# Low-rank stage: two-bank gelus, a moved output step, an x product on TensorE and a new split of the final sums

## The chip, the cores and the metric

The kernel runs on one core of a Trainium2 chip. The metric is device time in microseconds (us) from start to end of one execution. Before the change it is 999.62 us, the median of 3 runs (998.93 to 999.8).

A core has a matmul engine (TensorE, "PE" in the profile; "PEld" is its weight load), a vector engine (VectorE, "DVE"), an activation engine (ScalarE, "ACT"), a general engine (GpSimd, "POOL") and a sync engine (SyncE, "SP"). Each works through its own queue of instructions in order. Matmul results land in PSUM, which has eight banks of 128 partitions by 512 fp32 numbers here. Transfers to and from memory are issued by SP or ACT and run on 16 DMA engines.

## What is computed

Two layers with residuals over x of shape (32, 128, 128) in fp32:

```
x = x + L0_ffn(L0_cond(x, cond))     # mixtures of experts
x = x + L1_ffn(L1_cond(x, cond))
# L1_cond: shared silu experts + 8 routed gelu experts, weighted and summed
# L1_ffn, the low-rank stage:
P = x @ U1                 # 128 -> 32
H = gelu(P @ V1 + b1)      # 32 -> 512, tanh form of gelu
Q = H @ U2                 # 512 -> 32
out = Q @ V2 + b2          # 32 -> 128
```

The kernel folds U1 into the last weights of L1_cond, so that the experts' outputs are summed straight into P.

## The kernel before, in words

The 4096 tokens stand in 8 blocks (NB) of 512 columns (TB), with the 128 features on the partitions. Four blocks make a superblock (SB = 4), so there are two superblocks (NS = 2). All of x stays in SBUF (xT, later called x1T).

The work goes through stages. In L0 each shared unit (shared_up, L255) and each pair unit (pair_up, L429) multiplies into four PSUM tiles and takes a gelu of each (hidden, L239). Then comes the FFN: 8 blocks by 8 experts make 64 units (ffn_up, L615), each with four chunks. A chunk makes a tile g (gate) and a tile u (up) with by_columns (L217, matmul at L222); ScalarE takes silu of g (L569), VectorE multiplies it by u (L570). VectorE then forms four sums of the results (L630 to L633), and ffn_down (L640) projects.

In L1 the units stand in one list (`units`, L844 to L851): shared units "s", routed units "r" and low-rank units "l", each for a superblock. `pipelined` (L186) emits up(next unit), then down(this unit), then `after` for this unit.

A low-rank unit (sb, c) handles chunk c of the 512 hidden features for the four blocks of a superblock. low_up (L816) makes for each block a matmul with a contraction of 32 into its own PSUM tile ul, in its own quarter of the array's rows (L822), and a gelu of 128x512 (L823). low_down (L826) sums the four blocks' projections into the tile q_ps, a quarter of the array's columns each (`into`, L768, matmul at L771). When chunk 3 is done, low_out (L831) copies q_ps to qT (L833), multiplies by V2 for each block into o_ps (L837), adds b2 and x on VectorE (L839, tile fin), and stores: blocks 0 and 2 are issued on SyncE, blocks 1 and 3 on ScalarE (L841). The tail of the list runs: routed units 2 to 7 of superblock 1, then ("l", 0, 3), then the four ("l", 1, c). low_out(0) follows down("l", 0, 3), thus after up("l", 1, 0); low_out(1) comes last.

PSUM is shared out by tag: mm_tile (L107) gives one of six single-bank tiles in turn, y_tile (L110) one of two more for sums. A new tile of a tag waits until the last reader of an earlier one is done with it. The order of instructions on each engine is made by a planner: it follows program order as priority, and lets a later instruction go first when the earlier one is not ready in its own reckoning. It then sets every wait.

Of the kernel before, what the change touches and what calls it, by code (L numbers as in the profile page):

```python
# [44 lines left out]
SB = 4  # L45
NS = NB // SB
NT = B * S // P
H = 512
NC = H // P
# [28 lines left out]
def columns(cols):  # L78
    out, at = {}, 0
    for name, n in cols:  # L80
        out[name] = slice(at, at + n)
        at += n
    return out, at
# [3 lines left out]
AT32, NCOLS32 = columns(COLS32)  # L87
# [5 lines left out]
def adaln_ffn(  # L93
# [3 lines left out]
    nc = tc.nc  # L97
    V = nc.vector
# [4 lines left out]
    work = ctx.enter_context(tc.tile_pool(name="work", bufs=2))  # L103
    dram = ctx.enter_context(tc.tile_pool(name="dram", bufs=1, space=bass.MemoryType.DRAM))
    psum = ctx.enter_context(tc.tile_pool(name="psum", bufs=1, space=bass.MemoryType.PSUM))

    def mm_tile(name):  # L107
        return psum.tile([P, TB], F32, tag="mm", name=name, bufs=6)

    def y_tile(name):  # L110
        return psum.tile([P, TB], F32, tag="y", name=name, bufs=2)

    def const(shape, name, dtype=F32):
        return cpool.tile(shape, dtype, tag=name, name=name)
# [3 lines left out]
    par32 = const([P, NCOLS32], "par32")  # L118
# [11 lines left out]
    ident = const([P, P], "ident")  # L130
# [17 lines left out]
    for to, w in zip(downs_t, (s_w2, r_w2[: E1 // 2], r_w2[E1 // 2 :])):  # L148
        n = w.shape[0]
        nc.sync.dma_start(out=to.rearrange("p (e f) -> p e f", e=n), in_=w.rearrange("e d f -> d e f"))  # L150

    def col(name, i=0, n=1):
        return par[:, AT[name].start + i : AT[name].start + i + n]
# [85 lines left out]
    def hidden(ps, h, rhs, w, bias, unit):  # L239

        for c in range(NC):
            before("up", *unit, c)
            nc.tensor.matmul(ps[c], lhsT=w[:, c * P : (c + 1) * P], rhs=rhs, start=True, stop=True)  # L243
            nc.scalar.activation(h[:, c, :], ps[c], AF.Gelu_apprx_tanh, bias=bias[:, c : c + 1])  # L244
# [9 lines left out]

    def shared_up(blk):  # L255
        h = work.tile([P, NC, TB], F32, tag="h", name=f"hs0_{blk}", bufs=3)
        ps = [mm_tile(f"us_{blk}_{c}") for c in range(NC)]
        hidden(ps, h, xT[blk], sw1_t, col("sb1", 0, NC), ("s", blk))
        if blk < 2:
            for b in range(4 * blk, 4 * blk + 4):  # L260
                sums(b)
        return h
# [143 lines left out]
    def fetch(q):  # L406

        if q % 4 == 0:
            batch["e"] = registers(expert_at, q, mybir.EngineType.SP, (E0 - 1) * P)
        w = wpool.tile([P, NPCOLS], F32, tag=f"w{q % NW}", name=f"w_{q}")  # L410
        nc.sync.dma_start(out=w, in_=experts[bass.ds(batch["e"][q % 4], P), :])
        weights[q] = w
# [14 lines left out]
    def pair_up(q):  # L427
        if q + NW - 1 < NPAIR:
            fetch(q + NW - 1)  # L429
        if q + AHEAD < NPAIR:  # L430
            gather(q + AHEAD)
        w, x = weights[q], slots.pop(q)
        h = work.tile([P, NC, 2 * S], F32, tag="h", name=f"h0_{q}", bufs=3)
        ps = [mm_tile(f"u_{q}_{c}")[:, : 2 * S] for c in range(NC)]
        hidden(ps, h, x.rearrange("p s t -> p (s t)"), w[:, ATP["w1"]], w[:, ATP["eb1"]], ("p", q))
        return h

# [97 lines left out]
    held, in_dram, fgates = {}, {}, {}  # L535
# [64 lines left out]
    def gate_ahead(i):  # L600

        if i < len(ffn_units):
            blk, e = ffn_units[i]
            g, k = divmod(e, 4)
            bcast[i] = spread(fgates[blk][32 * k : 32 * k + 1, g, :], f"fg_{blk}_{e}")
# [9 lines left out]
    def ffn_up(blk, e):  # L615
        i = blk * EF + e
        gate_ahead(i + 2)
        input_ahead(i + 1)
        h = work.tile([P, NC, TB], F32, tag="h", name=f"hf_{blk}_{e}", bufs=3)
        cg = gated.pop((blk, e))  # L620
        for c in range(NC):
            cs = slice(c * P, (c + 1) * P)
            g, u = mm_tile(f"g_{blk}_{e}_{c}"), mm_tile(f"u_{blk}_{e}_{c}")
            by_columns(g, wg_t[:, e, cs], c0T[blk], D // 2)
            by_columns(u, wu_t[:, e, cs], cg, D // 2)
            glu(g, u, h[:, c, :], f"sf_{blk}_{e}_{c}")
        b11, b12, b21, b22 = (h[:, k, n] for k in (slice(0, 2), slice(2, 4)) for n in (slice(0, HALF), slice(HALF, TB)))
        t = work.tile([P, 3, 2, HALF], F32, tag="bsum", name=f"t_{blk}_{e}", bufs=2)
        t2, t3, t4 = (t[:, j] for j in range(3))
        V.tensor_tensor(t3, b22, b12, ALU.subtract)  # L630
        V.tensor_tensor(b12, b12, b11, ALU.subtract)  # L631
        V.tensor_tensor(t2, b22, b12, ALU.subtract)  # L632
        V.tensor_tensor(t4, t2, b21, ALU.subtract)  # L633
        if blk == 0:
            a_prepare(e)
        if rest:
            rest.pop(0)()
        return b11, b12, b21, b22, t2, t3, t4
# [115 lines left out]
    x1T = xT  # L754
# [13 lines left out]
    def into(y, w, h, first, last):  # L768

        for j in range(SB):  # L770
            nc.tensor.matmul(y[32 * j : 32 * (j + 1), :], lhsT=w, rhs=h[:, j, :], start=first, stop=last)  # L771

    def sh_up(sb, k):
        e, c = divmod(k, 2)
        h = work.tile([P, SB, TB], F32, tag="h", name=f"hs_{sb}_{k}", bufs=3)
        for j in range(SB):
            x = x1T[SB * sb + j]
            g, u = mm_tile(f"g1_{sb}_{k}_{j}"), mm_tile(f"u1_{sb}_{k}_{j}")
            by_columns(g, sws_t[0][:, e, c, :], x, 32)
            by_columns(u, sws_t[1][:, e, c, :], x, 32)  # L780
            glu(g, u, h[:, j, :], f"s1_{sb}_{k}_{j}")
        return h
# [13 lines left out]
    def r_up(sb, e):  # L796
        h = work.tile([P, SB, TB], F32, tag="h", name=f"hr_{sb}_{e}", bufs=3)
        g, k = divmod(e, 4)
        for j in range(SB):
            gate = spread(grows[sb][32 * k : 32 * k + 1, g, j * TB : (j + 1) * TB], f"rg_{sb}_{e}_{j}")  # L800
            ps = mm_tile(f"ur_{sb}_{e}_{j}")
            by_columns(ps, rw1_t[:, e, :], x1T[SB * sb + j], 32)
            a = work.tile([P, TB], F32, tag="sg", name=f"ar_{sb}_{e}_{j}", bufs=4)
            nc.scalar.activation(a, ps, AF.Gelu)  # L804
            V.tensor_tensor(h[:, j, :], a, gate, ALU.mult)  # L805
        return h
# [9 lines left out]
    def low_up(sb, c):  # L816
        h = work.tile([P, SB, TB], F32, tag="h", name=f"hl_{sb}_{c}", bufs=3)
        at = AT32["v1"].start + c * P
        for j in range(SB):
            ps = mm_tile(f"ul_{sb}_{c}_{j}")  # L820
            own = slice(32 * j, 32 * (j + 1))
            nc.tensor.matmul(ps, lhsT=par32[own, at : at + P], rhs=held["p", sb][own, :], start=True, stop=True)  # L822
            nc.scalar.activation(h[:, j, :], ps, AF.Gelu_apprx_tanh, bias=col("b1", c))  # L823
        return h

    def low_down(sb, c, h):  # L826
        if c == 0:
            held["q", sb] = y_tile(f"q_ps{sb}")
        into(held["q", sb], col("u2", c * 32, 32), h, c == 0, c == NC - 1)

    def low_out(sb):  # L831
        q = work.tile([P, TB], F32, tag="lgT", name=f"qT{sb}", bufs=1)
        V.tensor_copy(q, held["q", sb])  # L833
        for j in range(SB):
            ps = mm_tile(f"o_ps{sb}_{j}")
            own = slice(32 * j, 32 * (j + 1))
            nc.tensor.matmul(ps, lhsT=par32[own, AT32["v2"]], rhs=q[own, :], start=True, stop=True)  # L837
            t = work.tile([P, TB], F32, tag="fin", name=f"fin{sb}_{j}", bufs=4)
            V.scalar_tensor_tensor(t, ps, col("b2"), x1T[SB * sb + j], ALU.add, ALU.add)  # L839
            queue = nc.sync if j % 2 == 0 else nc.scalar  # L840
            queue.dma_start(out=out[SB * sb + j], in_=t)  # L841

    STAGES = {"s": (sh_up, sh_down), "r": (r_up, r_down), "l": (low_up, low_down)}
    units = [("s", sb, k) for sb in range(NS) for k in range(4)]  # L844
# [8 lines left out]
    def after(kind, sb, i):  # L853
        if (kind, sb, i) == ("s", 0, 0):
            gate_rows(0)

            l1_scores(1)
        if (kind, sb, i) == ("s", 0, 2):
            route(1)
        if (kind, sb, i) == ("s", 1, 0):  # L860
            gates_to_dram("r", 1)
            gate_rows(1)
        if kind == "r" and i == E1 - 1:
            low_in(sb)
        if (kind, sb, i) == ("l", 0, NC - 1):
            low_out(0)

    def unit_up(kind, *at):
# [4 lines left out]

    pipelined(units, unit_up, unit_down, after)
    low_out(1)


# [80 lines left out]
```

## Time and profile before

| What | us |
|---|---|
| median of 3 runs | 999.62 |
| the profiled execution, device time | 998.32 |
| its span, first to last record | 996.6 |
| TensorE matmul busy | 983.5 |
| VectorE busy | 634.3 |
| ScalarE busy | 353.2 |
| gelus of the low-rank stage (L823), 32 of 128x512, mean each | 0.696 |
| table loads on ScalarE for L823, 2, mean each | 1.283 |
| sums fin (L839), 8, mean each | 0.742 |
| silu in the FFN (L569), 256, mean each | 0.598 |
| product in the FFN (L570), 256, mean each | 0.686 |

In the profile a group of instructions is written as line, engine, operation, output <- inputs, shapes and count. In a timeline the first two columns are the start and the length in us; instructions of one group that follow each other are merged, and the brackets hold the idle time of the engine ahead of them and what ended it. "L841 ACTq" is the issue of a transfer from ScalarE's queue. Ends of matmuls are modelled, so starts are the better measure.

### The profile page before, as it was taken

Reading aid. Unit: us, or ns where it says so; the run is one execution under the profiler, and the core shown is the slowest. Engines: PE = TensorE matmul, PEld = TensorE weight load, DVE = VectorE, ACT = ScalarE, POOL = GpSimd, SP = SyncE. Lnnn points to the kernel's source line nnn. Section 1 sums busy time; section 2 is a strip of 40 time slices with the busy share of each in tenths; the row PEclk is TensorE's granted clock in tenths of the full one; section 3 lists DMA queues with packets and bytes.
Section 4 is the critical chain, followed back from the end, with each engine's and each line's share of the span. In section 5 each row is a group of like instructions: output and inputs, shape, how many; then the busy total and the mean of one; then the engine's idle time right before and its main releaser. Section 6 shows DMA issues by size and latency. Waiting matters only on the chain.

```text
span 996.6 us, 15169 instructions
## 1 busy us (share of the span) xinstructions
PE 983.5 (99%) x5998; PEld 465.0 (47%) x5998; DVE 634.3 (64%) x1126; ACT 353.2 (35%) x615; POOL 142.0 (14%) x145
## 2 busy tenths in 40 slices
PE   8999999999999999999999999999999999999996
PEld 3588886344444444444444444444444443323341
DVE  4444445667685676686676687668667656638593
ACT  5355445323232232232232323223223223335764
POOL 0000000210010101010101010101010001009780
PEclk9999999999999999999999999999999999999999
DMA  9555551000000000000000000000000000000002
GB/s 331 179 169 172 179 173 46 26 1 1 4 1 1 1 1 2 1 1 1 1 2 1 1 1 4 1 2 1 1 1 1 1 1 4 1 7 2 1 2 85
DMA packets 18743, 35.10 MB, mean 35 GB/s; under 512 B 1696, under 2 KB 9888, under 8 KB 18656
## 3 DMA queue, kind: packets, MB, share of 16 engines
q1 hardware_dynamic: 17808, 32.61, 10.3%
q10 hardware_dynamic: 864, 1.52, 0.4%
q8 instruction: 47, 0.77, 0.3%
q14 instruction: 24, 0.20, 0.1%
HBM read 31.76 MB, written 2.36 MB: 34 GB/s over the span
## 4 chain that ended last, share of the span: by engine, by line
PE 97%; DVE 2%; DMA 0%; issue 0%; DVEq 0%; POOL 0%
PE u L222 25%; PE g L222 25%; PE ya L656 10%; PE yb L656 8%; PE y L250 6%; PE u L243 6%; PE ur L222 6%; PE us L243 3%; PE ys L250 3%; PE p_ps L771 2%; PE ul L822 1%; PE q_ps L771 1%; DMA sw_t<-in_sw 0%; DVE hf L631 0%; PE fold_ps L233 0%; DVE t L632 0%
## 5 line engine op out<-in xcount | busy, mean ns | idle before, releaser
L569 ACT ACTIVATE sf<-g 128x512 f32<-128x512 f32 x256 | 152.8, 598 | 438.4 <-PE g L222 423.2
L570 DVE TENSOR_TENSOR hf<-sf,u 128x512 f32<-128x512 f32 x256 | 174.9, 686 | 185.6 <-PE u L222 185.0
L222 PE MATMUL g<-c0all,wg_t 128*64 128x512 f32 x1024 | 270.3, 593 | 0.0
L222 PE MATMUL u<-cg,wu_t 128*64 128x512 f32 x1024 | 270.1, 592 | 0.2 <-DVE cg L612 0.2
L564 POOL PARTITION_BROADCAST fg<-fgT x64 | 72.4, 1144 | 680.9 <-DVE cg L612 498.1
L222 PEld LDWEIGHTS u<-cg,wu_t 128*64 128x64 f32 x1024 | 75.6, 137 | 145.7 <-issue 124.1
L222 PEld LDWEIGHTS g<-c0all,wg_t 128*64 128x64 f32 x1024 | 75.7, 137 | 120.2 <-issue 108.2
L656 PE MATMUL ya<-t,wd_t 128*64 128x256 f32 x512 | 121.6, 379 | 0.1
L564 POOL PARTITION_BROADCAST rg<-grows x64 | 67.5, 1183 | 145.7 <-DVE hr L805 76.8
L244 ACT ACTIVATE h<-u,w 128x256 f32<-128x256 f32 x136 | 58.3, 474 | 63.1 <-PE u L243 61.5
L805 DVE TENSOR_TENSOR hr<-ar,rg 128x512 f32<-128x512 f32 x64 | 61.1, 1002 | 15.5 <-ACT ar L804 15.4
L656 PEld LDWEIGHTS ya<-t,wd_t 128*64 128x64 f32 x512 | 69.9, 137 | 0.7 <-DVE t L633 0.6
L656 PE MATMUL yb<-hf,a_sum 128*64 128x256 f32 x512 | 69.1, 379 | 0.0
L656 PE MATMUL ya<-t,a_sum 128*64 128x256 f32 x256 | 65.9, 379 | 0.0
L656 PE MATMUL ya<-hf,wd_t 128*64 128x256 f32 x256 | 65.8, 379 | 0.0
L250 PE MATMUL y<-h,w 128*128 128x256 f32 x272 | 64.3, 379 | 0.0
L243 PE MATMUL u<-x,w 128*128 128x256 f32 x272 | 64.1, 379 | 0.0
L631 DVE TENSOR_TENSOR hf<-hf 128x512 f32<-128x512 f32 x64 | 62.7, 979 | 2.1
L222 PE MATMUL ur<-xall,rw_t 128*32 128x512 f32 x512 | 58.4, 592 | 0.0
L250 PEld LDWEIGHTS y<-h,w 128*128 128x128 f32 x272 | 51.7, 190 | 7.5 <-DVE a_sum L592 0.2
L243 PEld LDWEIGHTS u<-x,w 128*128 128x128 f32 x272 | 51.7, 190 | 7.5 <-PE ys L250 0.2
L656 PEld LDWEIGHTS ya<-hf,wd_t 128*64 128x64 f32 x256 | 34.9, 137 | 42.8 <-issue 31.9
(204 smaller groups left out, 955.3 us busy)
## 6 DMA issues: line engine op xcount, KB each, us to landing
w<-in_experts SPq DMA_DIRECT2D x34, 578.5 KB
xall<-in_x SPq DMA_DIRECT2D x8, 256.0 KB
wg_t<-in_w_gate SPq DMA_DIRECT2D x8, 256.0 KB
wu_t<-in_w_up SPq DMA_DIRECT2D x8, 256.0 KB
wd_t<-in_w_down SPq DMA_DIRECT2D x8, 256.0 KB
out<-fin SPq DMA_DIRECT2D x4, 256.0 KB
out<-fin ACTq DMA_DIRECT2D x4, 256.0 KB
downs<-in_r_w SPq DMA_DIRECT2D x2, 256.0 KB
```

What stands on the lines that cost most here:

```text
L222: nc.tensor.matmul(ps[own, :], lhsT=w[:, own], rhs=x, start=True, stop=True)
L243: nc.tensor.matmul(ps[c], lhsT=w[:, c * P : (c + 1) * P], rhs=rhs, start=True, stop=True)
L244: nc.scalar.activation(h[:, c, :], ps[c], AF.Gelu_apprx_tanh, bias=bias[:, c : c + 1])
L250: nc.tensor.matmul(y[:, :n], lhsT=w[:, c, :], rhs=h[:, c, :n], start=(c == 0), stop=(c == NC - 1))
L564: nc.gpsimd.partition_broadcast(bc, row)
L569: nc.scalar.activation(s, ps_gate, AF.Silu)
L570: V.tensor_tensor(h, s, ps_up, ALU.mult)
L631: V.tensor_tensor(b12, b12, b11, ALU.subtract)
L656: nc.tensor.matmul(y[half, n], lhsT=w[:, c, :], rhs=h[:, c, :], start=False, stop=(e == EF - 1 and last))
L771: nc.tensor.matmul(y[32 * j : 32 * (j + 1), :], lhsT=w, rhs=h[:, j, :], start=first, stop=last)
L805: V.tensor_tensor(h[:, j, :], a, gate, ALU.mult)
L822: nc.tensor.matmul(ps, lhsT=par32[own, at : at + P], rhs=held["p", sb][own, :], start=True, stop=True)
```

## The change

PSUM tiles of the tag "mm" become pairs of banks, three of them in place of six single tiles. Users of two or four tiles draw whole pairs; a user of one tile takes a pair and leaves half of it unused. A low-rank gelu now reads two banks at once and writes two blocks of h (128x1024), and is pinned behind the ScalarE instruction traced ahead of it.

low_out(0) moves one unit later, behind down("l", 1, 0). low_out handles blocks 2 and 3 first, then 0 and 1. For superblock 0 all four sums stay on VectorE, and all four stores are issued on SyncE. For superblock 1, out_begin multiplies x of blocks 0 and 1 by the identity into a pair of banks, ahead of the last summation of q_ps; V2's product is added to it there, and ScalarE adds b2 (Identity with a bias) and issues these two stores. Blocks 2 and 3 stay with VectorE and SyncE.

```diff
+    def mm_pair(name):
+        return psum.tile([P, 2, TB], F32, tag="mm", name=name, bufs=3)
     def mm_tile(name):
-        return psum.tile([P, TB], F32, tag="mm", name=name, bufs=6)
+        return mm_pair(name)[:, 0, :]
+    def mm_tiles(name, n):
+        pairs = [mm_pair(f"{name}_{i}") for i in range(0, n, 2)]
+        return [t[:, i, :] for t in pairs for i in range(2)]
...
-        ps = [mm_tile(f"us_{blk}_{c}") for c in range(NC)]
+        ps = mm_tiles(f"us_{blk}", NC)
...
-            g, u = mm_tile(f"g_{blk}_{e}_{c}"), mm_tile(f"u_{blk}_{e}_{c}")
+            g, u = mm_tiles(f"gu_{blk}_{e}_{c}", 2)
...
     def low_up(sb, c):
-        for j in range(SB):
-            ps = mm_tile(f"ul_{sb}_{c}_{j}")
-            own = slice(32 * j, 32 * (j + 1))
-            nc.tensor.matmul(ps, lhsT=par32[own, at : at + P], rhs=held["p", sb][own, :], start=True, stop=True)
-            nc.scalar.activation(h[:, j, :], ps, AF.Gelu_apprx_tanh, bias=col("b1", c))
+        for j in range(0, SB, 2):
+            ps = mm_pair(f"ul_{sb}_{c}_{j}")
+            for i in range(2):
+                own = slice(32 * (j + i), 32 * (j + i + 1))
+                nc.tensor.matmul(
+                    ps[:, i, :], lhsT=par32[own, at : at + P], rhs=held["p", sb][own, :], start=True, stop=True
+                )
+            tc.keep_in_program_order(
+                nc.scalar.activation(h[:, j : j + 2, :], ps, AF.Gelu_apprx_tanh, bias=col("b1", c))
+            )
...
     def low_down(sb, c, h):
         if c == 0:
             held["q", sb] = y_tile(f"q_ps{sb}")
+        if (sb, c) == (NS - 1, NC - 1):
+            out_begin(sb)
         into(held["q", sb], col("u2", c * 32, 32), h, c == 0, c == NC - 1)
+    def out_begin(sb):
+        o = mm_pair(f"o_x{sb}")
+        for j in range(2):
+            nc.tensor.matmul(o[:, j, :], lhsT=ident, rhs=x1T[SB * sb + j], start=True, stop=False)
+        held["o", sb] = o
     def low_out(sb):
...
-        for j in range(SB):
-            ps = mm_tile(f"o_ps{sb}_{j}")
-            own = slice(32 * j, 32 * (j + 1))
-            nc.tensor.matmul(ps, lhsT=par32[own, AT32["v2"]], rhs=q[own, :], start=True, stop=True)
-            t = work.tile([P, TB], F32, tag="fin", name=f"fin{sb}_{j}", bufs=4)
-            V.scalar_tensor_tensor(t, ps, col("b2"), x1T[SB * sb + j], ALU.add, ALU.add)
-            queue = nc.sync if j % 2 == 0 else nc.scalar
-            queue.dma_start(out=out[SB * sb + j], in_=t)
+        begun = held.pop(("o", sb), None)
+        for first in (2, 0):
+            with_x = begun is not None and first == 0
+            o = begun if with_x else mm_pair(f"o_ps{sb}_{first}")
+            for i in range(2):
+                own = slice(32 * (first + i), 32 * (first + i + 1))
+                nc.tensor.matmul(
+                    o[:, i, :], lhsT=par32[own, AT32["v2"]], rhs=q[own, :], start=not with_x, stop=True
+                )
+            for i in range(2):
+                blk = SB * sb + first + i
+                t = work.tile([P, TB], F32, tag="fin", name=f"fin{blk}", bufs=4)
+                if with_x:
+                    nc.scalar.activation(t, o[:, i, :], AF.Identity, bias=col("b2"))
+                else:
+                    V.scalar_tensor_tensor(t, o[:, i, :], col("b2"), x1T[blk], ALU.add, ALU.add)
+                queue = nc.scalar if with_x else nc.sync
+                queue.dma_start(out=out[blk], in_=t)
...
-        if (kind, sb, i) == ("l", 0, NC - 1):
+        if (kind, sb, i) == ("l", 1, 0):
             low_out(0)
```

pair_up, sh_up and r_up draw their tiles with mm_tiles in the same way; r_up draws its two pairs ahead of its loop over the blocks.

More of the change, by code (lines that the diff above doesn't have):

```diff
@@ L433, in pair_up @@
         h = work.tile([P, NC, 2 * S], F32, tag="h", name=f"h0_{q}", bufs=3)
-        ps = [mm_tile(f"u_{q}_{c}")[:, : 2 * S] for c in range(NC)]
+        ps = [t[:, : 2 * S] for t in mm_tiles(f"u_{q}", NC)]
         hidden(ps, h, x.rearrange("p s t -> p (s t)"), w[:, ATP["w1"]], w[:, ATP["eb1"]], ("p", q))
@@ L777, in sh_up @@
             x = x1T[SB * sb + j]
-            g, u = mm_tile(f"g1_{sb}_{k}_{j}"), mm_tile(f"u1_{sb}_{k}_{j}")
+            g, u = mm_tiles(f"gu1_{sb}_{k}_{j}", 2)
             by_columns(g, sws_t[0][:, e, c, :], x, 32)
@@ L798, in r_up @@
         g, k = divmod(e, 4)
-        for j in range(SB):
+        ur = mm_tiles(f"ur_{sb}_{e}", SB)
+        for j, ps in enumerate(ur):
             gate = spread(grows[sb][32 * k : 32 * k + 1, g, j * TB : (j + 1) * TB], f"rg_{sb}_{e}_{j}")
-            ps = mm_tile(f"ur_{sb}_{e}_{j}")
             by_columns(ps, rw1_t[:, e, :], x1T[SB * sb + j], 32)
@@ L833, in low_out @@
         V.tensor_copy(q, held["q", sb])
-        for j in range(SB):
-            ps = mm_tile(f"o_ps{sb}_{j}")
-            own = slice(32 * j, 32 * (j + 1))
-            nc.tensor.matmul(ps, lhsT=par32[own, AT32["v2"]], rhs=q[own, :], start=True, stop=True)
-            t = work.tile([P, TB], F32, tag="fin", name=f"fin{sb}_{j}", bufs=4)
-            V.scalar_tensor_tensor(t, ps, col("b2"), x1T[SB * sb + j], ALU.add, ALU.add)
-            queue = nc.sync if j % 2 == 0 else nc.scalar
-            queue.dma_start(out=out[SB * sb + j], in_=t)
+        begun = held.pop(("o", sb), None)
[16 more added lines that the diff above has]
+                queue.dma_start(out=out[blk], in_=t)
     STAGES = {"s": (sh_up, sh_down), "r": (r_up, r_down), "l": (low_up, low_down)}
```

## The prediction

> **What bounds the kernel now.** I read the page first: busy shares, then the chain that ended last.
>
> ```profile
> PE 983.5 (99%) x5998; PEld 465.0 (47%) x5998; DVE 634.3 (64%) x1126; ACT 353.2 (35%) x615; POOL 142.0 (14%) x145
> ...
> PE 97%; DVE 2%; DMA 0%; issue 0%; DVEq 0%; POOL 0%
> ```
>
> TensorE carries 97% of the chain. Summing the stretches in which no matmul is on record gives 6.6 us up to the last matmul (4.8 of them at the start, before the first weights), and another 6.4 us of span follow it. None of the matmuls outside the last stage is shortened by the change, so a gain can only come from that stage, after about 969 us. There I read the timeline by engine.
>
> ```profile
> 970.57 2.42 ACT L823 ACTIVATE hl<-ul,par 128x512 f32<-128x512 f32 x4
> 973.87 2.42 ACT L823 ACTIVATE hl<-ul,par 128x512 f32<-128x512 f32 x4 [0.88 <-PE ul L822]
> 978.30 1.67 ACTq L841 DMA_DIRECT2D out<-fin  x2
> 980.01 7.09 ACT L823 ACTIVATE hl<-ul,par 128x512 f32<-128x512 f32 x12 [3.72 <-DVE fin L839]
> ...
> 976.86 2.72 DVE L839 SCALAR_TENSOR_TENSOR fin<-o_ps,par,xall 128x512 f32<-128x512 f32 x4 [1.21 <-PE o_ps L837]
> 988.24 0.69 DVE L833 COPY qT<-q_ps 128x512 f32<-128x512 f32 x1 [8.66 <-PE q_ps L771]
> 990.15 2.73 DVE L839 SCALAR_TENSOR_TENSOR fin<-o_ps,par,xall 128x512 f32<-128x512 f32 x4 [1.21 <-PE o_ps L837]
> ```
>
> ScalarE sits idle for 3.72 us: two stores of the first superblock are queued on it and wait for VectorE's sums (L839), and the gelus of the second superblock stand behind them. Then 12 gelus run without a pause to 987.10, and the end hangs on the last: q_ps complete and qT begun at 988.24, o_ps, four sums, stores, end 996.6. I call the start of qT "T"; from T to the end is 8.3 us. The third view is of the last stores, by windows (length, busy PE, PEld, DVE, ACT, POOL, clock, DMA share, GB/s).
>
> ```profile
> 991.00:992.00 1.00, 0.00 (x0) 0.00 (x0) 1.00 (x2) 0.00 (x0) 0.00 (x0) 0.88 0.23 86
> 992.00:993.00 1.00, 0.00 (x0) 0.00 (x0) 0.87 (x2) 0.00 (x0) 0.00 (x0) 0.50 1.02 383
> 993.00:994.00 1.00, 0.00 (x0) 0.00 (x0) 0.00 (x0) 0.00 (x0) 0.00 (x0) 0.50 1.00 381
> 994.00:995.00 1.00, 0.00 (x0) 0.00 (x0) 0.00 (x0) 0.00 (x0) 0.00 (x0) 0.50 0.52 199
> ```
>
> All 16 DMA engines are full from about 991.8 until the last byte: 0.23+1.02+1.00+0.52 = 2.77 us for the four stores.
>
> **Part by part.** *Gelus over two banks.* The 12 in a row give a step of (7.09-0.70)/11 = 0.58 us. The same line's 128x512 and 128x256 forms at L244 (687 and 474 ns) price 512 more columns at 0.43. A pair should therefore last 1.12 and step by 1.01, against 1.16 for two singles: eight pairs of the second superblock save 1.2 us, if ScalarE is never starved. Bounds: 0 (if crossing a bank costs the overlap) and 1.2.
>
> *Order, pairs of banks and queue.* The 3.72 us stall goes, but low_out(0) now takes two of three pair slots in the middle of the gelus. Call the second superblock's pairs p0 to p7. A group of matmuls takes 1.08 us of TensorE when the next is tiled the other way (ul at 972.71, q_ps at 973.78; q_ps at 982.38, ul at 983.46), and ul is ready 1.16 after its start (972.71 to 973.87).
> 1. p0, p1: gelus 973.87 to 976.00; they wait for pT, which nothing moves.
> 2. p2, p3: TensorE free at 974.9, p3's slot comes with p0's gelu at 975.0; ready 976.2, gelus to 978.3.
> 3. q_ps of chunk 0 at 976.1, o_ps of superblock 0 at 977.2 in the slots of p1 and p2, ready 978.4; sums (0.75, then 0.66 each) end at 979.1, 979.8, 980.4, 981.1.
> 4. p4 has to wait for p3's slot (978.3): ready 979.5, so ScalarE idles 1.2 us; gelu to 980.6. p5 waits for the second sum (979.8) and for q_ps of chunk 1 on TensorE to 980.4: ready 981.6, 1.0 us idle, gelu to 982.7. p6 and p7 follow without a wait: gelus to 984.75.
> 5. TensorE from 982.7 on: q_ps of chunk 2 (0.86), the two x products, q_ps of chunk 3 (0.86, and 0.28 to drain): T = 986.4.
> That is 988.24-986.4 = 1.8 us of gain. The four SyncE stores at 978 to 982 hold up nothing, since SP has no other work then.
>
> The Trainium skill, TensorEngine Tiling (Array Packing), Key Properties, says that changing the tiling mode drains the array; it speaks against splitting ul into pairs that wait separately. The row beside it: 1.08 for a group before a change of mode, 0.86 where the next has the same tiling (p_ps at 901.30, ur at 902.16), so 0.22 per change. If each pair were fenced off by changes, four more of them would add 0.9; by the rows I count them only where step 4 separates p4 and p5.
>
> *x of two blocks on TensorE.* Two 128x128 by 128x512 products, four records at the 0.43 us step of L243: 1.72 us. They need a slot, which comes with p5's gelu (982.7), so they land in the last stretch: q_ps of chunk 3 could begin at 984.8 by its gelus and begins at 985.3. Cost 0.5 to 0.6, already in step 5; bounds 0 (an earlier slot) and 1.7 (all in the way).
>
> *Sums split over two engines.* VectorE keeps two of four sums (1.4 instead of 2.73 us), ScalarE takes two at a copy's price (L678: 0.59; about 0.69 with a bias, as L244). The first store still needs qT, o_ps and one sum, T+2.7; only the later ones come sooner. The skill, DMA: Bandwidth & Descriptors, Issuing engines are not separate DMA queues, says that all queues run on the same 16 engines and that more issuers save only issue time. By the VectorE row alone the split would give 1.3 us; by rule and windows together nothing, for the stores already filled the engines from the first to the last. On ScalarE the second sum stands behind the first one's store issue (L841, 0.34), which full engines hide. I take 0; bounds 0 and 0.3 (one SP issue, L841 332 ns, off the first gap). A table switch for Identity is not priced: the Copy at L678 has no load of its own, and a load (L823, 1.28) would run before its operand is there.
>
> *Pairs elsewhere.* A lone tile now takes a pair, and g is held until VectorE has read u. I put each tile's first matmul against the end of the read that would free its slot in a pool of three. In the FFN:
>
> ```profile
> 407.44 0.69 DVE L570 TENSOR_TENSOR hf<-sf,u 128x512 f32<-128x512 f32 x1 [0.33 <-PE u L222]
> ...
> 410.59 1.03 PE L222 MATMUL g<-c0all,wg_t 128*64 128x512 f32 x4
> ```
>
> The chunk three later starts 2.46 us after its slot is free. All g/u pairs have at least 0.36 us, usually over 1.5. Before the last stage the pool falls short only at 19.2 to 19.6 us, where gate_ps, mod_ps and t_ps stand beside a shared chunk: 0.26 us short, taken as 0.1 on the path. Bounds: 0, since the exp behind them waits for its table load anyway (21.23 to 22.51), and 1.7, if mod_ps is put behind two shared products (1.72).
>
> **Sum.** -1.8 + 0.1 = -1.7 us. Against the profiled execution (998.32, of which 996.6 is the span) that is 996.6; the median shown is 1.3 us higher, 999.62, and becomes 997.9.
>
> **Rivals.**
> - *TensorE alone sets the end.* If slots never bind (o_ps later, or the x products earlier), TensorE from 972.71 has four ul and five q_ps groups, o_ps (ten of 1.08), and x: 12.5 us, T = 985.3; gain 2.9. For it: the sums and pairs leave TensorE gaps near 979. Against it: low_out stands ahead of p4 in the program. 999.62-2.9+0.1 = 996.8. Chance 0.30.
> - *The change doesn't do what it says*: ScalarE's queue stall merely becomes a slot stall. If all three slots are held until the sums at 981.1 and x is exposed fully (1.7), T = 986.4+1.5 = 987.9, time 999.4. For it: ul already waited on L839 in the profile. Chance 0.12.
> - *The pool of three holds up the FFN* (the slower side). The instruction order is planned afresh; if VectorE's four sums of an FFN unit (L630 to L633, 3.1 us) came ahead of the last L570, a pair would come free 3.1 us late. It decides from 2.46 us on: (3.1-2.46) x 64 units = 41 us, 1039. If that befell a tenth of the units, 1002. Against it: the margins above hold in the present order, and the diff moves no FFN operation. Chance 0.08.
>
> **Numbers.** The main case has 0.50, spread from 997.2 to 998.8. About 0.2% (2 us, so 997.6) is what a measurement here can tell from no change. Faster: the first rival's 0.30 and 0.12 of the main case, 0.42. Slower: 0.08. The rest, 0.50, is same. The range 996.2 to 999.7 leaves out the slower rival and the fringe of the first.
>
> **What would show it.** No store on ScalarE's queue before the end, and its 3.72 us idle replaced by two of about 1 us ending on ul; 16 two-bank gelus near 1.12 us; T near 986.4; the x products between the last two q_ps; the last stores again full for 2.8 us, though VectorE ends 1.3 us sooner. TensorE gaps inside the FFN, a third table load at L823, or T under 985.3 would prove me wrong.

## The result, and the profile after

The changed kernel takes 1023.08 us, the median of 4 runs (1022.28 to 1023.3), against 999.44 (4 runs) of the kernel before: a ratio of 1.0235, 95% interval 1.0218 to 1.0253. I had predicted 997.9. The profiled span is 1021.5 us against 996.6.

The page of the changed kernel shows the busy shares, the chain that ended last, and the routed experts' first product (tile ur), which no line of the diff touches except for where it draws its tiles:

```profile
PE 1006.9 (99%) x6002; PEld 465.8 (46%) x6002; DVE 603.2 (59%) x1124; ACT 350.5 (34%) x601; POOL 112.9 (11%) x145
...
PE 97%; DMA 1%; DVE 1%; issue 0%; DVEq 0%; POOL 0%; ACT 0%; POOLq 0%
...
L230 PE MATMUL ur<-xall,rw_t 128*32 128x512 f32 x512 | 78.1, 598 | 0.0
```

The same row on the page of the kernel before:

```profile
L222 PE MATMUL ur<-xall,rw_t 128*32 128x512 f32 x512 | 58.4, 592 | 0.0
```

TensorE is still "99% busy" and still carries 97% of the chain, so these two lines say nothing. The ur row does: the same 512 matmuls, 598 ns each instead of 592, cover 78.1 us instead of 58.4. Matmuls in different quarters of the array lie on top of each other on record, and the row counts such time once; they now overlap less. No idle time is booked for it.

Where the time went, by the starts of landmark instructions (differences of starts, each from one profiled execution; "write both" is the first experiment below):

| Stretch | before | after | difference | write both |
|---|---|---|---|---|
| start to the first FFN matmul | 186.2 | 188.9 | +2.7 | 186.9 |
| FFN | 643.2 | 644.9 | +1.6 | 643.4 |
| shared experts of L1 | 64.1 | 64.2 | +0.1 | 64.2 |
| first to last ur (routed experts, with three chunks of the first superblock's low-rank stage) | 74.5 | 96.9 | +22.4 | 75.1 |
| last ur to the second superblock's pT | 3.9 | 3.2 | -0.8 | 4.5 |
| pT to T (start of the last qT) | 16.3 | 15.0 | -1.2 | 15.0 |
| T to the last record's start | 8.3 | 8.4 | +0.1 | 8.4 |

The low-rank stage, to which I had given nearly all my working, did gain. Its timeline after the change:

```profile
1000.08 4.20 ACT L836 ACTIVATE hl<-ul,par 128x1024 f32<-128x1024 f32 x4 [0.50 <-PE ul L831]
...
1005.56 1.11 ACT L836 ACTIVATE hl<-ul,par 128x1024 f32<-128x1024 f32 x1 [1.29 <-PE ul L831]
...
1007.11 1.11 ACT L836 ACTIVATE hl<-ul,par 128x1024 f32<-128x1024 f32 x1 [0.44 <-PE ul L831]
...
1009.22 2.12 ACT L836 ACTIVATE hl<-ul,par 128x1024 f32<-128x1024 f32 x2 [1.00 <-PE ul L831]
...
1010.05 1.98 PE L852 MATMUL o_x<-xall,ident 128*128 128x512 f32 x4
...
1011.97 1.06 PE L779 MATMUL q_ps<-hl,par 128*32 128x512 f32 x8
...
1013.10 0.69 DVE L857 COPY qT<-q_ps 128x512 f32<-128x512 f32 x1 [5.91 <-PE q_ps L779]
...
1015.02 1.41 DVE L873 SCALAR_TENSOR_TENSOR fin<-o_ps,par,xall 128x512 f32<-128x512 f32 x2 [1.23 <-PE o_x L864]
1015.08 1.26 ACT L871 ACTIVATE fin<-o_x,par 128x512 f32<-128x512 f32 x2 [3.74 <-PE o_x L864]
```

The 3.72 us that ScalarE waited for VectorE's sums are gone; 1.29, 0.44 and 1.00 us of waiting for ul stand in their place. The x products lie between the last two q_ps groups. The windows of the last stores (columns as in the prediction):

```profile
1016.00:1017.00 1.00, 0.00 (x0) 0.00 (x0) 0.43 (x1) 0.35 (x1) 0.00 (x0) 0.82 0.37 139
1017.00:1018.00 1.00, 0.00 (x0) 0.00 (x0) 0.00 (x0) 0.00 (x0) 0.00 (x0) 0.50 1.02 373
1018.00:1019.00 1.00, 0.00 (x0) 0.00 (x0) 0.00 (x0) 0.00 (x0) 0.00 (x0) 0.50 1.01 385
1019.00:1020.00 1.00, 0.00 (x0) 0.00 (x0) 0.00 (x0) 0.00 (x0) 0.00 (x0) 0.50 0.43 152
```

The DMA engines are full for 0.37+1.02+1.01+0.43 = 2.83 us, before 2.77.

So the question is the routed stage. Its timeline of ScalarE, after the change:

```profile
926.31 1.08 ACT L812 ACTIVATE ar<-ur 128x512 f32<-128x512 f32 x2 [1.55 <-PE ur L230]
928.95 1.08 ACT L812 ACTIVATE ar<-ur 128x512 f32<-128x512 f32 x2 [1.55 <-PE ur L230]
```

and before:

```profile
929.02 0.60 ACT L804 ACTIVATE ar<-ur 128x512 f32<-128x512 f32 x1 [1.12 <-PE ur L222]
929.88 0.60 ACT L804 ACTIVATE ar<-ur 128x512 f32<-128x512 f32 x1 [0.26 <-PE ur L222]
930.74 0.60 ACT L804 ACTIVATE ar<-ur 128x512 f32<-128x512 f32 x1 [0.26 <-PE ur L222]
931.60 0.60 ACT L804 ACTIVATE ar<-ur 128x512 f32<-128x512 f32 x1 [0.26 <-PE ur L222]
```

A routed unit has four ur tiles. Before, their gelus start 0.86 us apart, and a unit (with its p_ps group) takes 4.29 us. After, two gelus start every 2.64 us, so a unit takes 5.28. There are 40 matmul records in a unit (32 of ur, 8 of p_ps). Before, four of them, one for each quarter of the array, start every 0.43 us: 10 steps, 4.29 us. 5.28 us are 12.3 such steps, so the quarters are no longer all filled. Of the 22.4 us, 14 steps from one unit to the next make 13.9; the step over the three low-rank chunks grew by 4.1 (from 11.26 to 15.34), and the last unit, whose ur now lie further apart, by 4.5. The waits of the weight loads name the partner (total us, times, longest), after the change:

```profile
PEld ur L230 <- ACT ar L812: 20.0, 56, 0.8
...
PEld us L251 <- ACT hs L252: 6.7, 10, 0.8
PEld u L251 <- ACT h L252: 5.1, 33, 0.2
```

The matmuls of ur, us and u, which are the users that were given tiles of two banks and read the first bank before they write the second, wait for the read on ScalarE. In the kernel before, the same view has 1.1 us for us and no line for ur or for the first layer's u. Which matmul waits is seen in the built program, in the order of TensorE's instructions (ur_1_0 is the pair of banks for blocks 0 and 1 of expert 1, four matmuls to a bank; the brackets name the engine whose progress is waited for):

```
Matmult ur_2_0_6044<-xall,rw_t 32x512 [waits Activation_49]
Matmult ur_1_0_6001<-xall,rw_t 32x512 [waits Activation_49]
Matmult ur_1_0_6001<-xall,rw_t 32x512 x3
Matmult p_ps_5481<-hr_0_5957,fold 32x512 [waits DVE_49]
Matmult ur_2_0_6044<-xall,rw_t 32x512 x3
```

The first matmul into the second bank of ur_1_0 waits for ScalarE: for the gelu of its own first bank. In the program r_up writes bank 0, reads it, writes bank 1, reads it. The waits are set by tile, and a pair of banks is one tile, so "write after read" holds between two banks that share no word. The planner then mixes the halves of neighbouring units into one another to fill the time, and does not quite succeed: a unit still takes 1 us longer.

### The profile page after: what moved, and what is told of

Read it like the earlier page. It is cut to its first block, busy times and chain, and to the rows that moved or that the text cites. A ratio compares the mean times of both kernels' runs of the same rounds, so it can differ in the third digit from the quotient of the medians.

```text
span 1021.5 us, 14899 instructions
## 1 busy us (share of the span) xinstructions
PE 1006.9 (99%) x6002; PEld 465.8 (46%) x6002; DVE 603.2 (59%) x1124; ACT 350.5 (34%) x601; POOL 112.9 (11%) x145
## 4 chain that ended last, share of the span: by engine, by line
PE 97%; DMA 1%; DVE 1%; issue 0%; DVEq 0%; POOL 0%; ACT 0%; POOLq 0%
PE gu L230 48%; PE ya L664 11%; PE yb L664 8%; PE ur L230 6%; PE u L251 6%; PE y L258 6%; PE us L251 3%; PE p_ps L779 3%; PE ys L258 2%; PE ul L831 1%; PE q_ps L779 1%; DMA fg<-fg_sb 0%; DMA sw_t<-in_sw 0%; PE fold_ps L241 0%; PE o_ps L864 0%; PE lg_ps L464 0%
## 5 line engine op out<-in xcount | busy, mean ns | idle before, releaser
L577 ACT ACTIVATE sf<-gu 128x512 f32<-128x512 f32 x256 | 152.7, 597 | 436.4 <-PE gu L230 433.5
L230 PE MATMUL gu<-cg,wu_t 128*64 128x512 f32 x1024 | 282.8, 592 | 0.4 <-DVE cg L620 0.4
L230 PE MATMUL gu<-c0all,wg_t 128*64 128x512 f32 x1024 | 283.2, 593 | 0.0
L578 DVE TENSOR_TENSOR hf<-sf,gu 128x512 f32<-128x512 f32 x256 | 175.2, 685 | 168.7 <-ACT sf L577 168.2
L230 PEld LDWEIGHTS gu<-cg,wu_t 128*64 128x64 f32 x1024 | 80.3, 137 | 144.6 <-issue 143.0
L230 PEld LDWEIGHTS gu<-c0all,wg_t 128*64 128x64 f32 x1024 | 80.2, 137 | 117.6 <-issue 100.9
L572 POOL PARTITION_BROADCAST fg<-fgT x64 | 51.5, 816 | 704.3 <-DVE cg L620 516.8
L230 PE MATMUL ur<-xall,rw_t 128*32 128x512 f32 x512 | 78.1, 598 | 0.0
L620 DVE TENSOR_TENSOR cg<-c0all,fg 128x512 f32<-128x512 f32 x64 | 45.3, 711 | 27.6 <-PE gu L230 26.4
L230 PE MATMUL gu<-xall,sws 128*32 128x512 f32 x512 | 58.3, 593 | 0.0
```

What stands on the lines that cost most here:

```text
L230: nc.tensor.matmul(ps[own, :], lhsT=w[:, own], rhs=x, start=True, stop=True)
L572: nc.gpsimd.partition_broadcast(bc, row)
L577: nc.scalar.activation(s, ps_gate, AF.Silu)
L578: V.tensor_tensor(h, s, ps_up, ALU.mult)
L620: V.tensor_tensor(t, c0T[blk], bcast.pop(i), ALU.mult)
```

## The experiments

All of them stand beside runs of the kernel before on the same chip.

| Run | median us | before beside it | ratio, 95% interval |
|---|---|---|---|
| 1 write both | 999.16 | 998.87 | 1.0003, 0.9994 to 1.0011 |
| 2 routed only | 1002.44 | 998.87 | 1.0033, 1.0021 to 1.0044 |
| 3 lone tiles | 999.02 | 998.87 | 1.0003, 0.9994 to 1.0012 |
| 4 pairs alone | 1050.13 | 998.87 | 1.0511, 1.0494 to 1.0529 |
| 5 single gelus | 999.63 | 998.59 | 1.0010, 1.0004 to 1.0017 |
| 6 no x | 998.83 | 998.59 | 1.0000, 0.9991 to 1.0008 |
| 7 no x, two queues | 998.41 | 998.80 | 0.9996, 0.9988 to 1.0005 |
| 8 no x, old place | 999.84 | 998.80 | 1.0009, 1.0001 to 1.0018 |
| 9 lone first layer | 1000.25 | 998.59 | 1.0017, 1.0009 to 1.0024 |
| 10 pairs alone, pinned | 1045.61 | 998.59 | 1.0467, 1.0451 to 1.0483 |
| 11 lone tiles, no x | 998.35 | 998.80 | 0.9995, 0.9986 to 1.0003 |
| 12 lone tiles in the FFN too | 1001.48 | 998.78 | 1.0026, 1.0018 to 1.0035 |

**1. Write both banks, then read both.** The changed kernel, with both matmuls of a pair put ahead of its two reads; the pool of pairs, the low-rank stage and everything else stay.

```diff
 in hidden:
-        for c in range(NC):
-            before("up", *unit, c)
-            nc.tensor.matmul(ps[c], ...)
-            nc.scalar.activation(h[:, c, :], ps[c], ...)
+        for p in range(0, NC, 2):
+            for c in (p, p + 1):
+                before("up", *unit, c)
+                nc.tensor.matmul(ps[c], ...)
+            for c in (p, p + 1):
+                nc.scalar.activation(h[:, c, :], ps[c], ...)
 in r_up:
-        for j, ps in enumerate(ur):
-            gate = spread(...)
-            by_columns(ps, ...)
-            ...
+        for p in range(0, SB, 2):
+            for j in (p, p + 1):
+                gates.append(spread(...))
+                by_columns(ur[j], ...)
+            for j, gate in zip((p, p + 1), gates):
+                ...
```

> The changed kernel, but in the first layer's hidden products and in the routed units both matmuls of a pair of banks are written before either bank is read. Theory 1 (a pair is one object to whatever sets the waits, so the second bank's matmul waited for the read of the first): the routed stage returns to 4.29 us per unit and gives back 22.4 us, the first layer 2.7; 1023.1-25.1 = about 998, at or a little under before. Theory 2 (a pool of three objects is too small, slots come free too late): as slow as the change, 1020 or more, for the pool is the same.

Measured: 999.16, ratio 1.0003. Within the interval, the whole loss of 23.6 us comes back. It does not end up under before: by the table above, the tail's gain (16.3 to 15.0) is spent in the routed stage (0.6), on the way to pT (0.6) and ahead of the FFN, where a single profile is uncertain by more than that (run 9). The order on TensorE, which had been the mixture above, is now plain:

```
Matmult p_ps_5481<-hr_0_5957,fold 32x512 [waits DVE_49] x4
Matmult ur_2_0_6044<-xall,rw_t 32x512 [waits PE_49,Activation_49]
Matmult ur_2_0_6044<-xall,rw_t 32x512 x7
Matmult ur_2_2_6045<-xall,rw_t 32x512 [waits PE_49,Activation_49]
Matmult ur_2_2_6045<-xall,rw_t 32x512 x7
```

The wait for ScalarE is still there, but it is for an older tile's read and long over. The wait that the change had made 20.0 us long is, by the same view of this run:

```profile
PEld ur L230 <- ACT ar L817: 0.3, 1, 0.3
```

A routed unit takes 4.29 us again.

**2. The same in the routed experts only.** The edit of r_up alone; `hidden` (first layer and pair experts) as in the change.

> The same, in the routed units alone. Theory 1: 1023.1-22.4 = about 1000.7, the first layer keeping its 2.7 us. Theory 2: 1020 or more.

Measured: 1002.44. Against run 1 this leaves 0.0030 of the time, 3 us, with the first layer; by the profiles the first FFN matmul starts 1.9 us later than in run 1, and the FFN lasts 0.7 us longer. The weight loads of us and u still wait 6.7 and 5.1 us for ScalarE, those of ur 0.3; in run 1 the view has no line for us or u. A single profile is uncertain by about 1.3 us ahead of the FFN (see run 9), but the four runs with the changed order in the first layer (the change and runs 2, 4 and 10) reach the FFN at 188.25 to 188.95 us, the ten others at 186.15 to 187.48. The first layer's share is a little larger than I had expected (2.7 us), the routed stage's smaller: some 20 us (1.0235 to 1.0033), not 22.4. Of the 21.8 us that first to last ur gives back (96.9 to 75.1), 1.3 are lost again on the way to pT (3.19 to 4.53).

**3. Lone tiles.** Here no pair is shared: each of us, u and ur takes one bank of a slot of its own. That leaves three such tiles at a time where the change had six, and it takes the common tile away without changing the order of the program.

```diff
-        ps = mm_tiles(f"us_{blk}", NC)
+        ps = [mm_tile(f"us_{blk}_{c}") for c in range(NC)]
 (the same for u in pair_up, and for ur in r_up, inside its loop)
```

> The changed kernel, but the first layer's hidden products and the routed units take a pair for each single tile and leave its second bank unused: three tiles in flight where there were six banks, and no two tiles share a pair. Theory 1: no shared pair, no wait, so within 3 us of 998. Theory 2: half the capacity of the change, so at least as slow as it, above 1023.

Measured: 999.02. Halving what the pool holds in these stages brings back as much as run 1. Too few slots, the rival, falls for these stages; two independent ways of taking the shared tile away give the same time.

**4. The pool of pairs, with the low-rank stage as before.** mm_tile and mm_tiles as in the change; low_up, low_down, low_out and the place of low_out(0) as in the kernel before.

> The pool of pairs alone: low-rank stage, place of low_out(0), stores and final sums as before the change. Theory 1: the loss is all in the pool, so 1023.1 plus the 1.2 us that the new tail gained, about 1024. Theory 3 (the low-rank stage's own edits cost the time, by switched tables or blocked queues): about 999.

Measured: 1050.13, 26 us over what I expected. My picture of independent parts fell here: without the pinned two-bank gelus the pool costs 51 us, not some 24. The groups of ScalarE in the last stretch of this run show one reason:

```profile
L812 ACT ACT_TABLE_LOAD x6 | 7.7, 1283 | 1.3 <-PE ur L230 1.2
L831 ACT ACT_TABLE_LOAD x6 | 7.7, 1283 | 0.1
```

Twelve table loads, where the changed kernel has two at each of its two lines: the two kinds of gelu take turns on ScalarE. That the planner orders them so because ur keeps it waiting is my reading.

**10. The same, pinned.** Run 4 with its low-rank gelus bound to the written order.

```diff
-            nc.scalar.activation(h[:, j, :], ps, AF.Gelu_apprx_tanh, bias=col("b1", c))
+            tc.keep_in_program_order(
+                nc.scalar.activation(h[:, j, :], ps, AF.Gelu_apprx_tanh, bias=col("b1", c))
+            )
```

> Base: the version with the pool of pairs and the low-rank stage as before (1050.13, 26 us over the change, with 12 table loads in place of 4). Here its single gelus of the low-rank stage are bound to the written order, nothing else. Theory (the 26 us are the gelus of two kinds taking turns on ScalarE, each turn a table load, because the planner was free to mix them): the table loads fall to 4 and the time to 1024 to 1027, the loss of the pool alone. Rival (the lone tiles of the low-rank stage in a pool of three slots, and the stores queued on ScalarE, cost it whatever the order): over 1040.

Measured: 1045.61. The table loads fall to four, as expected, and that is worth only 4.5 us. The other 21 us or so have another cause, so my theory falls and the rival holds. From pT to T this run takes 31.9 us, the change 15.0; of the rest, 4.0 us lie between the first and the last ur and 1.7 after T. Its timeline from pT to T:

```profile
1015.13 1.27 ACT L832 ACTIVATE hl<-ul,par 128x512 f32<-128x512 f32 x2 [7.33 <-DVE fin L849]
...
1021.84 1.84 ACT L832 ACTIVATE hl<-ul,par 128x512 f32<-128x512 f32 x3 [3.17 <-PE ul L830]
1022.58 2.07 PE L830 MATMUL ul<-pT,par 32*128 32x512 f32 x2 [0.77 <-ACT hl L832]
1024.58 1.94 PE L779 MATMUL q_ps<-hl,par 128*32 128x512 f32 x8
```

ScalarE idles 7.33 us until a sum of low_out(0), where before it idled 3.72. The four ul products of a chunk lie in four quarters of the array; before, a group of all four took 1.14 us (at 972.71). With three slots the fourth waits for the first one's gelu and then runs alone, and ScalarE waits 3.17 us for the next three. The windows add another loss (the column before the last two is the granted clock):

```profile
1003.00:1011.00 8.00, 6.35 (x25) 1.43 (x24) 1.38 (x2) 3.27 (x6) 0.00 (x0) 0.87 0.00 0
1011.00:1023.00 12.00, 10.44 (x26) 3.60 (x24) 2.82 (x4) 3.80 (x7) 0.00 (x0) 0.50 0.23 87
1023.00:1035.00 12.00, 11.17 (x34) 1.87 (x33) 0.00 (x0) 3.90 (x7) 0.00 (x0) 0.50 0.00 1
```

The clock goes to half at about 1009 us (0.87 over the first 8 us) and stays there; a q_ps group takes 1.94 us instead of 1.06. How the 16.9 us by which this stretch is longer than in the changed kernel divide between slots, the stores on ScalarE's queue and clock was not separated.

**5. Two gelus for each pair.** Run 1 with a single gelu for each bank, pinned.

```diff
-                nc.scalar.activation(h[:, j : j + 2, :], ps, ...)
+            for i in range(2):
+                    nc.scalar.activation(h[:, j + i, :], ps[:, i, :], ...)
```

> Base: the version with both matmuls of a pair written first (999.16; T, the start of the last qT, at 989.06 and span 997.5). Here each two-bank gelu of the low-rank stage becomes two 128x512 gelus on the same pair, in the written order; all else stays. Theory (the two-bank gelu is what gains in the tail): from pT1 to T ScalarE runs eight gelus of 0.696 us for four of 1.112 us, 1.12 us more, and the stage of 14.95 us goes back towards the 16.27 us of before: 1000.2. Rival (the gain comes from the order of the work alone, the stores and low_out(0) out of ScalarE's way): the stage stays at 15.0 us and the time at 999.2.

Measured: ratio 1.0010 against 1.0003 of run 1; the intervals overlap. From pT to T it takes 15.25 us, 0.3 more than run 1, where theory said 1.1 and the rival nothing. (This stretch repeats well where its code is the same: 14.95 us in runs 1, 2 and 9, 14.34 in runs 6 and 7.) So of the 1.3 us that this stretch gained over before, the two-bank gelu brings 0.3 and the rest of the change 1.0, the cost of x included. Of the profile's other difference to run 1, 0.6 us lie ahead of the FFN, where the two have the same instructions (see run 9).

**6. No x on TensorE.** Run 1 without out_begin: VectorE makes all sums, SyncE issues all stores.

> Base: the version with both matmuls of a pair written first (999.16). Here x is no longer added on TensorE: all four sums of the last superblock are VectorE's, and all its stores leave by SyncE. My prediction's step (x costs 0.5 to 0.6 us exposed on TensorE, the split of the sums gives nothing): T 0.5 us earlier, T to the end 8.3 to 8.5 us, 998.6. Rival (the split was worth what it cost): T 0.5 us earlier, but the last two sums and stores come late by the same, 999.2.

Measured: 998.83; pT to T 14.34 us, 0.6 less than run 1; T to the last record 8.27, against 8.37. The x products cost what I had said, and the split of the sums that they allow gives nothing back.

**7. The last stores on two queues.** Run 6, with every second store of the last superblock on ScalarE.

```diff
-                queue = nc.scalar if with_x else nc.sync
+                queue = nc.scalar if sb == 1 and i == 1 else nc.sync
```

> Base: the version with both matmuls of a pair written first and no x on TensorE (998.83 beside 998.59 of before; T to the end 8.27 us). Here the last superblock's second store of each pair leaves by ScalarE's queue, as in before; nothing else moves. My step (the last four stores take 2.8 us because the DMA engines are full, whichever engine issues them): T to the end 8.2 to 8.5 us, 998.8. Rival (one issuing engine spaces the stores out, two would start the last one sooner): 0.3 to 0.6 us less, 998.3.

Measured: 998.41; T to the last record 8.28 us, the same as in run 6. Which engine issues the last stores makes no difference here.

**8. The old place of low_out(0).** Run 6, with low_out(0) again behind ("l", 0, 3); its stores stay on SyncE.

```diff
-        if (kind, sb, i) == ("l", 1, 0):
+        if (kind, sb, i) == ("l", 0, NC - 1):
```

> Base: pairs written first, no x on TensorE (998.83 beside 998.59). Here the first superblock's last step is back ahead of the last superblock's second chunk, with its four stores still on SyncE alone. Theory A (the gain in the tail came from the stores leaving ScalarE's queue and from pairs, not from the place): the stage from pT1 to T stays at 14.3 to 14.6 us, 998.8. Theory B (the place matters: the second chunk's pairs then wait for the sums of the first superblock on VectorE, as the 3.72 us of ScalarE did in before): the stage is 15.3 to 16.3 us, 999.8 to 1000.8.

Measured: 999.84; pT to T 15.32 us, 1.0 more. ScalarE in run 6:

```profile
981.55 1.11 ACT L841 ACTIVATE hl<-ul,par 128x1024 f32<-128x1024 f32 x1 [1.29 <-PE ul L836]
983.12 1.11 ACT L841 ACTIVATE hl<-ul,par 128x1024 f32<-128x1024 f32 x1 [0.45 <-PE ul L836]
985.24 2.12 ACT L841 ACTIVATE hl<-ul,par 128x1024 f32<-128x1024 f32 x2 [1.00 <-PE ul L836]
```

and with the old place:

```profile
980.45 1.11 ACT L841 ACTIVATE hl<-ul,par 128x1024 f32<-128x1024 f32 x1 [2.07 <-PE ul L836]
982.22 1.11 ACT L841 ACTIVATE hl<-ul,par 128x1024 f32<-128x1024 f32 x1 [0.65 <-PE ul L836]
984.32 4.19 ACT L841 ACTIVATE hl<-ul,par 128x1024 f32<-128x1024 f32 x4 [0.99 <-PE ul L836]
```

Theory B holds: moved one unit earlier, low_out(0) takes its two slots while only two gelus of the second superblock are out of the way, and four are left to run at the end instead of two. The idle times in these lines add up to 2.74 us in run 6 and 3.71 here.

**9. Lone tiles in the first layer only.** Run 1 with us and u as in run 3 and `hidden` as before.

> Base: the version with both matmuls of a pair written first (999.16). Here the first layer and the gap between the pairs take lone tiles (one bank of a pair's slot each, three at a time) in the order of before; FFN, routed stage and low-rank stage stay as in the base. Theory (what is left of the loss in front is the pair as one object): the FFN starts at 186.2, where the lone-tile version had it and before too, not 186.9, and the gain carries to the end: 998.5. Rival (three tiles at a time in the first layer move the order of the work by chance, and the FFN gives it back, as it did with lone tiles, 1.2 us): 999.1 to 999.5.

Measured: 1000.25, worse than runs 1 and 3, which neither theory had. Its instructions up to the routed stage are those of run 3 on every engine, and yet its profile has the first FFN matmul at 187.48 us and that of run 3 at 186.15. What a single profile shows ahead of the FFN is therefore good to about 1.3 us only, and the 0.7 us by which run 1 starts its FFN later than before can't be put down to the change. The routed and low-rank stages of run 9 take 0.9 us more than those of run 3. The remaining 0.5 us or so by which its ratio is higher stays open.

**11. Lone tiles, no x.** Runs 3 and 6 together.

> The lone-tile version (first layer, pairs' gap and routed stage with one bank of a pair each; 1.0003 of before, T at 988.47) without x on TensorE. What the runs have shown adds up to: routed stage and step to pT1 as in before (74.8 and 3.7 us), low-rank stage 14.4 us as without x, T to the end 8.3; 0.5 us under the lone-tile version, a ratio of 0.9995 to 1.0000, 998.4 where before is 998.6 to 999.0. Rival (the front of the lone-tile version was an accident of one execution, and it costs like the run with the lone first layer, 1.0017 with x): 999.5 to 999.8.

Measured: 998.35, ratio 0.9995 with an interval up to 1.0003. It is the best version found, and not measurably better than the kernel before. From pT to T it takes 14.64 us, 1.6 less than before; its FFN, with g and u in pairs, takes 644.5 us, 1.3 more.

**12. Lone tiles in the FFN too.** Run 11 with g and u each in a slot of its own.

```diff
-            g, u = mm_tiles(f"gu_{blk}_{e}_{c}", 2)
+            g, u = mm_tile(f"g_{blk}_{e}_{c}"), mm_tile(f"u_{blk}_{e}_{c}")
```

> Base: lone tiles in first layer and routed stage, no x on TensorE (998.35 beside 998.8 of before). Here g and u of the FFN are lone tiles too, so that three of them are alive where before had six; only the low-rank stage and the last sums still use two banks of a slot. My prediction's slot step (the read that frees a slot of three ends 2.46 us before the FFN's matmul that takes it): the FFN lasts 643 to 645 us as in all runs so far, 998.4. The prediction's slower rival (three slots hold up the FFN, where the planner lets g and u of the next group wait): several us in the FFN, 1002 or more.

Measured: 1001.48, ratio 1.0026. The FFN takes 647.3 us, 2.8 more than in run 11. The waits of the weight loads name VectorE's product, in total and at two of their longest:

```profile
PEld g L230 <- DVE hf L578: 44.1, 124, 0.9
...
280.85 0.20 PEld L230 LDWEIGHTS g<-c0all,wg_t 128*64 128x64 f32 x4 [0.93 <-DVE hf L578]
282.79 0.20 PEld L230 LDWEIGHTS g<-c0all,wg_t 128*64 128x64 f32 x4 [0.88 <-DVE hf L578]
```

The loss is not spread over the 64 units. Against run 11 it comes in steps of some 0.5 us, one in the second unit of each block but the first, and reaches 3.7 us at the last unit; 0.9 us come back at the end of the FFN (see the next section). In these second units the products stand on VectorE among the last sums of the block before (L691 to L707); in the other units no such wait is over 0.4 us, and next to no time is lost. So a pool that holds three such tiles does hold up the FFN, where VectorE has other work between the products. In the changed kernel it holds six, and the same wait adds up to 2.0 us, none over 0.3.

## Why the prediction was wrong, point by point

**The step that failed** is "Pairs elsewhere". I had put "each tile's first matmul against the end of the read that would free its slot in a pool of three", and found 0.36 us or more to spare. That is the wait for a slot. It leaves out a wait inside the slot, and so put it at nothing: when a tile of two banks is written, read, written and read, the second write waits for the first read. Runs 1 and 3 remove this wait in two ways and each return to the time of before; run 2 divides it: some 20 us (1.0235 to 1.0033) in the routed stage, some 3 us (1.0033 to 1.0003) ahead of it. I could have read it off the diff: r_up draws its pairs ahead of a loop that multiplies and reads block by block, hidden does the same, while ffn_up writes g and u before it reads either. The Trainium skill, Perfetto Trace Analysis, Matmuls, advises rotating matmul groups through different banks so that the read of one overlaps the next group's matmuls; the banks here were different, and in the routed stage the overlap was still lost, because the waits follow the tile.

**"None of the matmuls outside the last stage is shortened"** was true and misleading. I drew from it that a gain can only come from the last stage, and never asked with the same care what the other 970 us could lose. The diff touched all of them.

**The FFN.** I said that it would be unharmed; it takes 1.6 us longer. Its offset to before is 2.73 us at its first gate matmul, about 3.6 from the sixth unit on, 3.47 at the last gate matmul and 4.37 at the last matmul of all: 0.7 us go at the start, 0.9 at the end, and the pace between is that of before. The end is the same mechanism seen from the other side, a read of one half that waits for the write of the other. In the built program silu of g waits for the last matmul of u, where before it waited for that of g. So what VectorE's product waits for last is no longer u but silu (before, then after):

```profile
L570 DVE TENSOR_TENSOR hf<-sf,u 128x512 f32<-128x512 f32 x256 | 174.9, 686 | 185.6 <-PE u L222 185.0
L578 DVE TENSOR_TENSOR hf<-sf,gu 128x512 f32<-128x512 f32 x256 | 175.2, 685 | 168.7 <-ACT sf L577 168.2
```

Inside the FFN this harms nothing. Behind the last unit TensorE has to wait for the sums made from it: from the last gate matmul to the last matmul of the FFN it is 7.89 us before, 8.79 in the change and in runs 1, 3 and 11, and again 7.89 in run 12, where g and u are apart. Why the start loses 0.7 us was not settled.

**The slower rival** had the right sign and the wrong place: it named the FFN and a tile that comes free late, at 1002 or 1039. Run 12 shows what a tile that comes free late is worth when it does occur: some 0.5 us in each block, 2.8 us in all.

**Gelus over two banks.** Predicted 1.12 us and a step of 1.01; measured 1.11 and, for two in a row, 2.12-1.11 = 1.01. The saving of 1.2 us was tied to "if ScalarE is never starved". It is starved, and run 5 puts it at 0.3.

**Order and queue.** I predicted 14.4 us from pT to T (986.4-971.97), measured 15.0. The pairs p0 to p3 and p4 came as worked out (idle 1.2 predicted, 1.29 measured), p5 idled 0.44 instead of 1.0, but p6 and p7 did not "follow without a wait": q_ps of chunk 1 stood ahead of their ul on TensorE, and ScalarE idled 1.00 us. That 14.4 came near 15.0 is in part luck: 0.6 us too much at p5 stand against 1.0 too little at p6. The gain of 1.8 us was thus 1.2. In run 8 the place of low_out(0) alone is worth 1.0 of it.

**x on TensorE.** Predicted 0.5 to 0.6 us exposed; run 6 gives 0.6. **Sums split over two engines.** Predicted to give nothing; T to the end is 8.3 us before, 8.4 after, 8.27 and 8.28 in runs 6 and 7. Both steps held.

**The evidence I had named** was half right: "TensorE gaps inside the FFN" would not have shown it, for the loss was in another stage, and it left no gap on record.

## What to carry to other kernels

When two buffers are joined into one tile, go through every user of that tile and list its writes and reads in program order: wherever a read of one half stands ahead of the write of the other, the write now waits for the read, even though they share nothing. Write all parts before reading any, or keep the tiles apart. Written first, the halves still have one price: the first read waits for the last write. And when a change touches a shared helper, cost its effect on all callers by their share of the time, not by where the gain is meant to be.

## What the runs showed that I had not expected

TensorE lost a fifth of its pace in the routed stage with its busy share unchanged. The page books no idle time for ur; what tells it is the busy time of one group over the same count of instructions (58.4 to 78.1 us), or the period of the engine that reads the results (4.29 to 5.28 us).

The granted clock fell to 0.50 in run 10 while TensorE was still at work in short groups: no idle stretch of TensorE on record between 1003 and 1012 us is longer than 0.9 us, but it started 25 matmuls in the 8 us before the fall (1001 to 1009), where the changed kernel started 46 in 8 us of the same stage (998 to 1006) and kept a clock of 1.00 to its last matmul groups:

```profile
1005.00:1013.00 8.00, 7.52 (x44) 1.76 (x40) 2.20 (x4) 4.34 (x4) 0.00 (x0) 1.00 0.36 133
```

What the clock goes by, these runs do not separate.

The same instructions, built into two kernels that differ only later, reached the FFN 1.3 us apart in two profiles.
